# One tanh result left in its PSUM bank, and a list plan that knows the shared SBUF port

## Chip, core and metric

The kernel runs on one core of a Trainium2 chip. The metric is the device time of one execution in microseconds. PE is TensorE (matmuls), DVE is VectorE, ACT is ScalarE, POOL is GpSimd, and SP is the engine whose queue issues nearly all transfers (DMA).

## The reference, cut to what matters

The input x has 64 batches of 256 nodes with 128 features, in fp32. Four graph layers follow each other, each wrapped as a residual with a layernorm. All share one symmetric 256 x 256 adjacency matrix.

```
x = layernorm(x + attention0(x, adj))      # softmax over axis 1, plus x @ self_weight
x = layernorm(x + attention1(x, adj))      # softmax over masked leaky scores, then elu
x = layernorm(x + gated(x, adj, steps=5))  # see below
x = layernorm(x + chebyshev(x, adj, 3))    # adj^1, adj^2, adj^3 times x, then a weight

# one of the five steps of gated(); in_matrix and out_matrix are both adj
m_in = m_out = adj @ h
av = concat(m_in, m_out)
u3 = h @ u3_w.T + u3_b
z  = sigmoid(av @ w3_w.T + w3_b + u3)
r  = sigmoid(av @ w4_w.T + w4_b + u3)
hv = tanh(av @ w5_w.T + w5_b + ((r * h) @ u5_w.T + u5_b))
h  = (1 - z) * h + z * hv
```

## The kernel before, in words

**Units and lanes.** Two batches make a unit, so there are 32 units. Ten lanes, each with its own SBUF tiles, hold ten units in flight at once. A unit goes through `layer0` to `layer3` in its lane, and when it is done the lane starts the unit ten further on.

**A state update (layer2).** A unit's five updates each do the following.

1. `left_fast` multiplies by the adjacency in a scheme with seven block products in place of eight. `block_sums` (L833, L835, L836) forms sums of blocks, for these layers on GpSimd. Two banks, `x` and `y`, take the products (PE L844). Two small ScalarE copies (L856 and L859, 128 x 128) stand inside this chain, since a copied partial result is accumulated further in the same bank. Then VectorE merges (L865, and L875, L877, L878 in `merged`) into the tile m.
2. `product` (PE L902) adds up the gate inputs in the bank `ps_g` and those of candidate v in the bank `ps_v`, both 512 columns wide.
3. ScalarE takes three tanh: r's (L914), z's (L922), candidate v's (L931). Sigmoids are written through tanh with scales, so no table changes.
4. VectorE does four `scalar_tensor_tensor`: r times h (L917), (z - 1) times h (L929), (z + 1) times v (L933), and the difference that is the new state (L935). Here v is the product of candidate v.
5. The new state is turned back to node-major form. For most steps VectorE transposes 32 x 32 blocks (L943), SP writes the result to the HBM buffer hb (L946) and reads it back in another order into ht (L949, four transfers). At the first and last units some turns go through TensorE (L968) and a ScalarE copy (L971).

In the groups of the profile, r and z stand under the tile name e and v under p, because they share those tiles' memory.

**Other lines named below.** L351 are warm-up matmuls. In `layer0` and `layer1`: L576 spreads a row to all partitions with TensorE, L667 and L743 are matmuls of layer 0, L674 and L698 small and wide VectorE steps, L773 masks the attention weights and L780 uses them, L783 and L792 follow. L533 turns x by TensorE and L535 copies it out. L546, L549 and L552 turn x through HBM. L592 is the power -0.5 on GpSimd in every layernorm, L611 the normalisation on ScalarE. L314 loads x, L654 transposes it for later units. L821 are plain adjacency products. L1004 and L1015, and at the last three units L1051, L1055 and L1058, belong to layer 3. L629 to L642 are the layernorm and the output of the last units.

**The order.** No engine's order is written by hand. `Plan.add` records every operation as a task, with an engine, an estimated duration in ns, and the cells it reads and writes. `Plan.run` then goes through a planned time: each engine, when free, takes from its ready tasks the one with the smallest key, and the instructions are issued in that order. Each engine then executes its own list strictly in order, and semaphores hold an instruction until its inputs are there. So the plan's times only set the order; the run's times are the chip's.

What shapes the order:

- `LATENCY` is added after a task before a task on another engine may count on it; `EARLY` takes its place in the first 35 us of planned time. `OWN` is the same for a task on its own engine.
- The eight PSUM banks are handed out by the plan. A task that takes a bank is only chosen when one is free, and a bank is free when its last user has ended.
- The key `first` is the unit's number times `PERIOD` plus the task's due time within its unit, which `PACE` (or `PACE_GATED` in layer 2) stretches. For the last ten units `LATE` and `TAIL` bring the units closer together. `HASTE` is taken off the key of a task that uses a bank without taking it.

Of the kernel before, what the change touches and what calls it, by code (L numbers as in the profile page):

```python
# [13 lines left out]
P = 128  # L14
# [6 lines left out]
BL = 32  # L21
# [11 lines left out]
PERIOD = 46000.0  # L33
TAIL = 0.3
LATE = 6
PACE = 3.0
PACE_GATED = 1.65
HOLD = 80
DIRECT_ROWS = 3
XDIRECT = 10  # L40
START = 35e3
HASTE = {"pe": 10000.0, "act": 10000.0, "dve": 10000.0}
PLAIN = 3
# [17 lines left out]
class Task:  # L61
    def __init__(self, eng, ns, fn, unit, wait, dma):
        self.eng, self.ns, self.fn, self.unit, self.wait, self.dma = eng, ns, fn, unit, wait, dma
        self.step, self.layer = 0, 0
        self.deps, self.then, self.left, self.at = set(), [], 0, 0.0
        self.off = self.end = self.due = 0.0
        self.banks, self.takes = [], []


class Plan:  # L70
# [4 lines left out]

    LATENCY = {"pe": 500, "dve": 400, "act": 400, "pool": 500, "sp": 3500}

# [9 lines left out]

    def add(self, eng, ns, fn, reads=(), writes=(), after=(), wait=0, group=None, dma=False):
        t = Task(eng, ns, fn, self.unit, wait, dma or eng == "sp")
        for c in reads:  # L90
            t.deps.update(c.writers)
            c.readers.append(t)
        for c in writes:
            if c.bank and not c.writers:
                t.takes.append(c)
            if group is None or c.group is not group:
                c.waits = {w for o in (c, *c.over) for w in (*o.writers, *o.readers)} - {t}
                c.writers, c.readers, c.group = [], [], group
            t.deps.update(c.waits)
            if c.bank and c.writers:  # L100

                t.deps.add(c.writers[0])
            c.writers.append(t)
        t.deps.update(after)
        t.deps.discard(t)
        for c in {id(c): c for c in (*reads, *writes) if c.bank}.values():
            c.users += 1
            t.banks.append(c)
        t.step = self.step = self.step + 1
        t.layer = self.layer  # L110
        t.rank = self.rank
        self.tasks.append(t)
        return t

    def seen_at(self, t, by):
        return t.end if t.eng != by.eng or t.dma else t.off + self.OWN[t.eng]

    def run(self, spawn, units, key):

        queue, done_at, order = list(units), {}, []  # L120
        open_units, lane_of = {}, {}
        ready = {e: [] for e in ("pe", "dve", "act", "pool", "sp")}
        free = dict.fromkeys(ready, 0.0)
        seen, now, running = 0, 0.0, []

# [15 lines left out]
        def start(lane):  # L141
            mine = [u for u in queue if u % LANES == lane]
            if mine:
                self.unit, self.step = mine[0], 0
                queue.remove(self.unit)
                lane_of[self.unit] = lane
                spawn(self.unit, lane)

                for t in self.tasks[seen:]:
                    t.due = max([d.due + (PACE_GATED if t.layer == 2 else PACE) * (d.ns + (  # L150
                        d.wait + self.LATENCY["sp" if d.dma else d.eng] if d.dma or d.eng != t.eng else self.OWN[t.eng]))
                        for d in t.deps if d.unit == t.unit], default=0.0)
                enlist()

# [3 lines left out]
        while any(ready.values()) or running:  # L158
# [10 lines left out]
            for e, tasks in ready.items():  # L169
# [4 lines left out]
                if not fit:  # L174
                    continue
                t = min(fit, key=key)
                if t.at > now:
# [4 lines left out]
                order.append(t)  # L182
                free[e] = t.off = now + t.ns
                t.end = t.off + (self.EARLY if now < START else self.LATENCY)["sp" if t.dma else e] + t.wait
# [19 lines left out]
def kernel(  # L204
# [315 lines left out]
    def small(u, what, ns, op, reads, writes, **more):  # L520

        pool = u >= TIGHT and what in SMALL
        add(POOL if pool else DVE, 300 if pool else ns, lambda: op(nc.gpsimd if pool else nc.vector), reads, writes, **more)

# [55 lines left out]
    def layernorm(u, L, pairs, swap=False, centred=False):  # L580
# [5 lines left out]
        for k, (c, view) in enumerate(pairs):  # L586
# [4 lines left out]
            op0=ALU.mult, op1=ALU.add), (st,), (ve,))  # L591
        add(POOL, 1150, lambda: nc.gpsimd.tensor_tensor(rstd.ap, ve.ap, nhalf.ap, op=ALU.pow), (ve, nhalf), (rstd,))  # L592
        by_act = u >= TIGHT and plan.layer in NORM

        if by_act and not centred:
            mean = st.ap.rearrange("p k (j s) -> p k j s", j=2)[:, :, :, 1]
            if "shift" in SMALL:
                add(POOL, 330, lambda: nc.gpsimd.tensor_scalar_mul(
                    nm.ap.rearrange("p (k j) -> p k j", k=2), mean, -1.0), (st,), (nm,))
                add(POOL, 250, lambda: nc.gpsimd.tensor_mul(ve.ap, nm.ap, rstd.ap), (nm, rstd), (ve,))  # L600
            else:
# [47 lines left out]
    def layer0(u, L):  # L649
# [47 lines left out]
        for b in range(UB):  # L697
            add(DVE, 540, lambda b=b: nc.vector.tensor_add(  # L698
                ev[:, b, :, 0:P].rearrange("p k (c i) -> p k c i", c=NC), rv()[:, b].rearrange("p c (i k) -> p k c i", k=2),
                neg0.ap[:, :, 0:P].rearrange("p k (c i) -> p k c i", c=NC)), (row, neg0), (e,), group=es)  # L700
        for b in range(UB):
# [22 lines left out]
        if not SCALES or u < TIGHT:  # L724
            add(DVE, 700, lambda: nc.vector.tensor_mul(
                h.ap[:, :, 0 : D + 2], h.ap[:, :, 0 : D + 2],
                rs.ap.rearrange("p (g o) -> p g o", o=1).to_broadcast([P, G, D + 2])), (h, rs), (h,))
        esd, rstd = L["esd"], L["rstd"]
# [27 lines left out]
    def layer1(u, L):  # L756
# [6 lines left out]
        for bs in [[b] for b in range(UB)] if u < HALVES else [list(range(UB))]:  # L763
# [3 lines left out]
            for b in bs:  # L767
# [6 lines left out]
                p.ap[:, at].rearrange("p (b c) n -> p b (c n)", b=n), e.ap[:, at].rearrange("p (b c) n -> p b (c n)", b=n),  # L774
                mask1.ap.rearrange("p (o c) n -> p o (c n)", o=1).to_broadcast([P, n, NC * N])), (ec, mask1), (pc,))

# [34 lines left out]
        xf = X[u].ap.rearrange("p b c d -> p (b c d)")  # L811
        add(DVE, 600, lambda: nc.vector.scalar_tensor_tensor(hp.ap, ex.ap, 1.0, hp.ap, op0=ALU.min, op1=ALU.max), (ex, hp), (hp,))
        add(DVE, 630, lambda: nc.vector.tensor_add(hp.ap, hp.ap, xf), (hp, X[u]), (hp,))
        layernorm(u, L, y_pairs(hp))


# [8 lines left out]
    def block_sums(src, blk, s, by_pool):  # L825
# [4 lines left out]
        by, eng = (POOL, nc.gpsimd) if by_pool else (DVE, nc.vector)  # L830
        wide, narrow = (780, 580) if by_pool else (350, 215)

        add(by, wide, lambda: eng.tensor_sub(  # L833
            four[:, 0:2], blk(slice(2, 3)).to_broadcast([P, 2, D]), blk(slice(0, 4, 3))), (src,), (s,), group=ss)
        add(by, narrow, lambda: eng.tensor_sub(four[:, 2:3], four[:, 1:2], blk(slice(0, 1))), (src, s), (s,), group=ss)  # L835
        add(by, narrow, lambda: eng.tensor_add(four[:, 3:4], four[:, 2:3], blk(slice(1, 2))), (src, s), (s,), group=ss)  # L836
        return four
# [42 lines left out]
    def layer2(u, L):  # L880
        h, ht = turned(u, L, -1), X[u]
        for step in range(STEPS):
# [18 lines left out]
            def product(ps, w, c, rhs, start, stop, after=()):  # L901
# [11 lines left out]
            up = part if step else 1.0  # L913
            add(ACT, 590, lambda ps_g=ps_g, up=up: nc.scalar.activation(  # L914
                r.ap, ps_g.ap, AF.Tanh, bias=bias2.ap[:, 1:2], scale=0.5 / up), (ps_g, bias2), (r,))
            tanh_r = list(r.writers)
            add(DVE, 650, lambda h=h: nc.vector.scalar_tensor_tensor(r.ap, r.ap, 1.0, h.ap, op0=ALU.add, op1=ALU.mult),  # L917
                (r, h), (r,))
            product(ps_v, lambda: gT.ap[:, 2], gT, m, True, False, tanh_r)
            product(ps_g, lambda: gT.ap[:, 0], gT, m, False, True)  # L920
            product(ps_v, lambda: u5T.ap[:, 0], u5T, r, False, True)
            add(ACT, 590, lambda ps_g=ps_g, up=up: nc.scalar.activation(  # L922
                z.ap, ps_g.ap, AF.Tanh, bias=bias2.ap[:, 0:1], scale=0.5 / up), (ps_g, bias2), (z,))

            new = L["xT1" if h is L["xT0"] else "xT0"]
            if not step:
                add(ACT, 600, lambda h=h, new=new, part=part: nc.scalar.mul(new.ap, h.ap, part), (h,), (new,))
                h = new
            add(DVE, 650, lambda h=h, new=new: nc.vector.scalar_tensor_tensor(  # L929
                new.ap, z.ap, -1.0, h.ap, op0=ALU.add, op1=ALU.mult), (z, h), (new,))  # L930
            add(ACT, 590, lambda ps_v=ps_v, up=up: nc.scalar.activation(  # L931
                v.ap, ps_v.ap, AF.Tanh, bias=bias2.ap[:, 2:3], scale=1 / up), (ps_v, bias2), (v,))
            add(DVE, 650, lambda: nc.vector.scalar_tensor_tensor(v.ap, z.ap, 1.0, v.ap, op0=ALU.add, op1=ALU.mult),  # L933
                (v, z), (v,))
            add(DVE, 650, lambda new=new, part=part: nc.vector.scalar_tensor_tensor(  # L935
                new.ap, v.ap, part, new.ap, op0=ALU.mult, op1=ALU.subtract), (v, new), (new,))
            h = new
# [35 lines left out]
        if far(u, STEPS - 1):  # L973
            add(DVE, 600, lambda: nc.vector.tensor_add(
                y.ap.rearrange("p (g a i) -> p g a i", g=G, i=BL), ht.ap.rearrange("p (a g i) -> p g a i", g=G, i=BL),
                X[u].ap.rearrange("p b c (a i) -> p (b c) a i", i=BL)), (ht, X[u]), (y,))
        else:
# [99 lines left out]
    def first(t):  # L1077
        if t.rank is not None:
            return t.rank * PERIOD
        if t.unit < 0:  # L1080
            return t.due - 1e6
        soon = HASTE.get(t.eng, 0) if t.banks and not t.takes else 0
        return (t.unit if t.unit < NU - LANES else NU - 1 - LATE - (NU - 1 - t.unit) * TAIL) * PERIOD + t.due - soon

# [33 lines left out]
```

The softmax here doesn't subtract the row's maximum and nothing guards it: scores larger than these inputs give would overflow.

## Time and profile before

| | |
|---|---|
| median of 5 runs | 1388.79 us (1388.35 to 1391.1) |
| the profiled execution | 1388.35 us, its span 1386.4 us |
| TensorE clock granted | 0.999 |
| busy, share of span | PE 99%, DVE 86%, ACT 68%, POOL 45% |
| transfers | 47.1% of 16 DMA engines on the main queue, 105 GB/s of HBM traffic |

The span runs from the first to the last instruction of the profile; about 2 us of the execution's own time lie around it. A matmul of fp32 stands as two rows in the profile (a transpose by TensorE as one)[...]. The interval from one row's start to the next one's tells what TensorE is really occupied with. In a groups line the first number is the busy time, the second the mean duration in ns, and what follows the bar is the idle time of the engine just before. A line of waits names the waiting engine and line, the one waited for, the total us, the number of times, and the longest.

### The profile page before, as it was taken

The numbers are of one execution on the slowest core, as the hardware profiler recorded it, in microseconds if no ns is written. First come the engines' busy times: TensorE is split into PE (matmuls) and PEld (weight loads), VectorE is DVE, ScalarE is ACT, GpSimd is POOL, SyncE is SP. The second block draws the span as 40 slices with busy tenths as digits, with TensorE's granted clock in tenths as the row PEclk, the third lists the DMA queues.
The fourth block names the chain that finished last, engine by engine and source line by source line (L and its number), as shares of the span: only waits on it lengthen the run. The fifth ranks groups of instructions, "written<-read, shape, count | busy, mean of one in ns | idle before, by whom it ended". The sixth has DMA issues, their size and how long they took to land.

```text
span 1386.4 us, 23294 instructions
## 1 busy us (share of the span) xinstructions
PE 1378.4 (99%) x6891; PEld 965.9 (70%) x6891; DVE 1195.2 (86%) x2745; ACT 943.0 (68%) x2303; POOL 626.5 (45%) x1039
## 2 busy tenths in 40 slices
PE   9999999999999999999999999999999999999998
PEld 8776666766666766676776777777676666667777
DVE  7888898998888898888988798899888888998865
ACT  6887556665766777766687678887766655565544
POOL 4134343534355454455354454465444533535433
PEclk9999999999999999999999999999999999999999
DMA  4224544554555554554545555445454454554322
GB/s 132 35 50 101 117 105 105 113 124 111 113 119 108 110 127 101 120 114 107 116 108 115 118 118 117 107 112 121 107 131 97 104 108 94 113 124 114 82 65 61
DMA packets 530077, 147.13 MB, mean 106 GB/s; under 512 B 456480, under 2 KB 495136, under 8 KB 529952
## 3 DMA queue, kind: packets, MB, share of 16 engines
q1 hardware_dynamic: 529152, 145.13, 47.1%
q8 instruction: 55, 0.90, 0.3%
q14 instruction: 70, 0.57, 0.2%
q10 hardware_dynamic: 800, 0.52, 0.1%
HBM read 81.10 MB, written 64.46 MB: 105 GB/s over the span
## 4 chain that ended last, share of the span: by engine, by line
PE 95%; DVE 3%; issue 0%; DMA 0%; POOL 0%; ACT 0%; SPq 0%; POOLq 0%; DVEq 0%; ACTq 0%
PE ps L902 48%; PE ps L844 20%; PE ps L1004 7%; PE ps L743 4%; PE ps L780 4%; PE ps L1015 3%; PE ps L738 2%; PE ps L667 2%; PE ps L792 2%; PE ps L821 1%; PE ps L1051 1%; DMA ht<-hb 0%; PE ps L1058 0%; DVE p L546 0%; PE ps L351 0%
## 5 line engine op out<-in xcount | busy, mean ns | idle before, releaser
L902 PE MATMUL ps<-m,gT 128*128 128x512 f32 x960 | 478.8, 593 | 0.0
L902 PEld LDWEIGHTS ps<-m,gT 128*128 128x128 f32 x960 | 166.0, 191 | 113.1 <-issue 91.1
L833 POOL TENSOR_TENSOR e<-ht 128x256 f32<-128x256 f32 x121 | 102.3, 845 | 213.6 <-DMA ht<-hb 160.1
L844 PEld LDWEIGHTS ps<-adjTp,ht 128*128 128x128 f32 x726 | 124.0, 191 | 82.5 <-issue 72.4
L914 ACT ACTIVATE e<-ps,bias 128x512 f32<-128x512 f32 x160 | 109.8, 686 | 95.2 <-PE ps L902 90.7
L931 ACT ACTIVATE p<-ps,bias 128x512 f32<-128x512 f32 x160 | 109.7, 685 | 85.6 <-PE ps L902 82.5
L902 PE MATMUL ps<-e,u5T 128*128 128x512 f32 x320 | 163.2, 593 | 0.0
L592 POOL TENSOR_TENSOR rstd<-ve,nhalf 128x4 f32<-128x4 f32 x126 | 143.1, 1137 | 36.3 <-DVE ve L589 31.3
L589 POOL TENSOR_SCALAR ve<-st 128x4 f32<-128x4 f32 x110 | 38.3, 349 | 258.4 <-DVE st L587 230.2
L844 PE MATMUL ps<-adjTp,e 128*128 128x128 f32 x968 | 149.6, 275 | 0.0
L922 ACT ACTIVATE e<-ps,bias 128x512 f32<-128x512 f32 x160 | 109.8, 687 | 55.4 <-PE ps L902 55.2
L844 PEld LDWEIGHTS ps<-adjTp,e 128*128 128x128 f32 x968 | 130.5, 192 | 13.8 <-issue 11.1
L844 PE MATMUL ps<-adjTp,ht 128*128 128x128 f32 x726 | 138.9, 275 | 0.2 <-DMA ht<-hb 0.2
L933 DVE SCALAR_TENSOR_TENSOR p<-e,p 128x512 f32<-128x512 f32 x160 | 114.1, 714 | 20.1 <-ACT p L931 19.5
L902 PEld LDWEIGHTS ps<-e,u5T 128*128 128x128 f32 x320 | 58.9, 190 | 63.8 <-issue 49.3
L611 ACT ACTIVATE x<-ht,ve,rstd 128x128 f32<-128x128 f32 x212 | 92.3, 489 | 14.0 <-POOL ve L600 14.0
L902 PE MATMUL ps<-xT,gT 128*128 128x512 f32 x192 | 98.0, 593 | 0.0
L875 DVE TENSOR_TENSOR m<-ps,m 128x256 f32<-128x256 f32 x182 | 74.8, 411 | 18.6 <-PE ps L844 17.3
L833 POOL TENSOR_TENSOR e<-x 128x256 f32<-128x256 f32 x61 | 48.6, 797 | 92.0 <-ACT x L611 78.6
L769 ACT ACTIVATE e<-m,esd 128x256 f32<-128x256 f32 x116 | 84.3, 767 | 0.2 <-DMA m<-row 0.2
L917 DVE SCALAR_TENSOR_TENSOR e<-e,xT 128x512 f32<-128x512 f32 x96 | 67.9, 708 | 16.5 <-ACT e L914 15.7
L844 PEld LDWEIGHTS ps<-adjT,x 128*128 128x128 f32 x366 | 60.7, 191 | 29.2 <-issue 24.3
(211 smaller groups left out, 3198.8 us busy)
## 6 DMA issues: line engine op xcount, KB each, us to landing
hb<-p SPq DMA_DIRECT2D x182, 256.0 KB, 2.4
ht<-hb SPq DMA_DIRECT2D x484, 64.0 KB, 2.5
xT<-hb SPq DMA_DIRECT2D x244, 64.0 KB, 2.6
m<-row SPq DMA_DIRECT2D x58, 256.0 KB, 3.8
hb<-p SPq DMA_DIRECT2D x124, 64.0 KB, 1.8
ht<-hb SPq DMA_DIRECT2D x31, 256.0 KB, 2.9
out_dram<-x SPq DMA_DIRECT2D x30, 256.0 KB, 2.5
m<-in_x_dram SPq DMA_DIRECT2D x88, 64.0 KB, 2.4
```

Source lines behind the costliest of these rows:

```text
L592: add(POOL, 1150, lambda: nc.gpsimd.tensor_tensor(rstd.ap, ve.ap, nhalf.ap, op=ALU.pow), (ve, nhalf), (rstd,))
L611: add(ACT, 400, lambda j=j, b=b, ch=ch, view=view, at=at, shift=shift, col=col: nc.scalar.activation(X[u].ap[:, b, ch, :], view()[:, j, :] ...
L769: add(ACT, 660 if u >= DIRECT_ROWS else 360, lambda g=g, b=b: nc.scalar.activation(e.ap[:, g, :].rearrange("p (c n) -> p c n", c=NC), ev() ...
L833: add(by, wide, lambda: eng.tensor_sub(four[:, 0:2], blk(slice(2, 3)).to_broadcast([P, 2, D]), blk(slice(0, 4, 3))), (src,), (s,), group=ss)
L844: add(PE, mm_ns(P) + 4, lambda: nc.tensor.matmul(ps.ap[:, at * P : (at + 1) * P], lhs(), mat.ap[:, k, c * P : (c + 1) * P], start=start, s ...
L875: add(DVE, 335, lambda: nc.vector.tensor_tensor(mv[:, 1:3], pv(y)[:, 0:2], mv[:, 3:4].to_broadcast([P, 2, P]), op=ALU.add), (y, m), (m,))
L902: add(PE, mm_ns(T), lambda: nc.tensor.matmul(ps.ap, w(), rhs.ap, start=start, stop=stop, skip_group_check=True), (c, rhs), (ps,), after)
L914: add(ACT, 590, lambda ps_g=ps_g, up=up: nc.scalar.activation(r.ap, ps_g.ap, AF.Tanh, bias=bias2.ap[:, 1:2], scale=0.5 / up), (ps_g, bias2 ...
L922: add(ACT, 590, lambda ps_g=ps_g, up=up: nc.scalar.activation(z.ap, ps_g.ap, AF.Tanh, bias=bias2.ap[:, 0:1], scale=0.5 / up), (ps_g, bias2 ...
L931: add(ACT, 590, lambda ps_v=ps_v, up=up: nc.scalar.activation(v.ap, ps_v.ap, AF.Tanh, bias=bias2.ap[:, 2:3], scale=1 / up), (ps_v, bias2), ...
L933: add(DVE, 650, lambda: nc.vector.scalar_tensor_tensor(v.ap, z.ap, 1.0, v.ap, op0=ALU.add, op1=ALU.mult), (v, z), (v,))
L1004: add(PE, mm_ns(N), lambda k=k, src=src, c=c, b=b, ps=ps, at=at: nc.tensor.matmul(gd(ps.ap)[:, at], bn(src.ap)[:, b, c * P : (c + 1) * P], ...
```

## The change

**Candidate v's tanh.** `IN_PSUM = (0, 0, 1, 0)` says for four values of an update (r's tanh, z's tanh, v's tanh, v's product) whether they stay in PSUM. Only the third does: ScalarE's tanh (L931 before, L968 after) writes over its own bank `ps_v` in place of the SBUF tile v. VectorE's product (L933 before, L971 after) reads the bank and writes the tile v. In the text of the update the last product into `ps_g` now stands ahead of the first product into `ps_v`.

**The plan.** Tasks have a mark `port` where VectorE reads two tensors of SBUF, and every GpSimd task has it. The plan starts a marked task on one of the two engines only when the other's marked task has let go. `TURN` puts a second marked VectorE task in a row behind unmarked ones whose keys are within 1000. VectorE's durations in units are multiplied by 1.03.

**Reserves, pace and haste.** `LATENCY` is shorter for pe, dve and act and longer for pool and sp. `HASTE` is now also taken off pool and sp tasks. It no longer goes to all tasks that use a bank without taking it, but to those that lie, in their unit's chain of dependences, between two uses of one bank (`hold`). `PACE`, `PACE_GATED`, `TAIL` and `LATE` have other values. Estimated durations are set anew: GpSimd's small steps at 180 to 195, its power at 1010, its sums at 705 and 435, VectorE's updates at 600.

The matrices, the tiling, the split of work between the engines and which turns go through HBM are the same. Cut to its core:

```diff
-TAIL = 0.3
-LATE = 6
-PACE = 3.0
-PACE_GATED = 1.65
+TAIL = 0.4
+LATE = 5
+PACE = 4.0
+PACE_GATED = 1.8
...
-HASTE = {"pe": 10000.0, "act": 10000.0, "dve": 10000.0}
+HASTE = {"pe": 10000.0, "act": 10000.0, "dve": 10000.0, "pool": 10000.0, "sp": 10000.0}
+IN_PSUM = (0, 0, 1, 0)
+MARGIN = {"dve": 1.03}
+TURN = 1000.0
...
-    LATENCY = {"pe": 500, "dve": 400, "act": 400, "pool": 500, "sp": 3500}
+    LATENCY = {"pe": 400, "dve": 350, "act": 350, "pool": 700, "sp": 4000}
...
+    def hold(self, tasks):
+        bits = {}
+        for t in tasks:
+            own = 0
+            for c in t.banks:
+                own |= bits.setdefault(id(c), 1 << len(bits))
+            t.after = t.before = own
+        for t in tasks:
+            for d in t.deps:
+                if d.unit == t.unit:
+                    t.after |= d.after
+        for t in reversed(tasks):
+            for d in t.deps:
+                if d.unit == t.unit:
+                    d.before |= t.before
+        for t in tasks:
+            t.within = bool(t.after & t.before) and not t.takes
...
-                t = min(fit, key=key)
+                t = min(fit, key=lambda t: key(t) + (TURN if twice and t.port and e == "dve" else 0))
...
-                free[e] = t.off = now + t.ns
+                begin = now
+                if t.port:
+                    begin = max(now, held["pool" if e == "dve" else "dve"])
+                free[e] = t.off = begin + t.ns
+                if e == "dve":
+                    twice = t.port
+                if t.port:
+                    held[e] = t.off - 65 if e == "dve" else begin + 50 if t.ns > 900 else t.off - 125
...
-        wide, narrow = (780, 580) if by_pool else (350, 215)
+        wide, narrow = (705, 435) if by_pool else (335, 211)
...
-            product(ps_v, lambda: gT.ap[:, 2], gT, m, True, False, tanh_r)
             product(ps_g, lambda: gT.ap[:, 0], gT, m, False, True)
+            product(ps_v, lambda: gT.ap[:, 2], gT, m, True, False, tanh_r)
...
+            tz, tv = ps_g if IN_PSUM[1] else z, ps_v if IN_PSUM[2] else v
...
-            add(ACT, 590, lambda ps_v=ps_v, up=up: nc.scalar.activation(
-                v.ap, ps_v.ap, AF.Tanh, bias=bias2.ap[:, 2:3], scale=1 / up), (ps_v, bias2), (v,))
-            add(DVE, 650, lambda: nc.vector.scalar_tensor_tensor(v.ap, z.ap, 1.0, v.ap, op0=ALU.add, op1=ALU.mult),
-                (v, z), (v,))
+            add(ACT, 590, lambda ps_v=ps_v, up=up, tv=tv: nc.scalar.activation(
+                tv.ap, ps_v.ap, AF.Tanh, bias=bias2.ap[:, 2:3], scale=1 / up), (ps_v, bias2), (tv,))
+            vv = (v, ps_g, ps_v)[IN_PSUM[3]]
+            add(DVE, 600, lambda tz=tz, tv=tv, vv=vv: nc.vector.scalar_tensor_tensor(
+                vv.ap, tz.ap, 1.0, tv.ap, op0=ALU.add, op1=ALU.mult), (tv, tz), (vv,), port=not (IN_PSUM[1] or IN_PSUM[2]))
...
-        soon = HASTE.get(t.eng, 0) if t.banks and not t.takes else 0
+        soon = HASTE.get(t.eng, 0) if t.within else 0
```

## The prediction

> **What bounds the kernel now.** I read the page's busy times first, then the TensorE clock, then the chain that ended last, then TensorE's own waits.
>
> ```profile
> PE 1378.4 (99%) x6891; PEld 965.9 (70%) x6891; DVE 1195.2 (86%) x2745; ACT 943.0 (68%) x2303; POOL 626.5 (45%) x1039
> ...
> PEclk9999999999999999999999999999999999999999
> ...
> PE 95%; DVE 3%; issue 0%; DMA 0%; POOL 0%; ACT 0%; SPq 0%; POOLq 0%; DVEq 0%; ACTq 0%
> ```
>
> TensorE (PE) is busy for 99% of the span at full clock, and it is 95% of the chain. But a row lasts longer than the interval to the next row, so "busy" can hide small stalls. The chain in order of time gives the intervals:
>
> ```profile
> 1.34 3.78 PE ps L351 x8
> ...
> 145.72 4.29 PE ps L902 x10
> ...
> 156.50 3.12 PE ps L844 x28
> ...
> 1372.32 3.45 PE ps L1058 x16
> ```
>
> Ten 512-column rows take 4.29, so one takes 0.429 us. A 128-column row takes 3.12/28 = 0.111 and a 256-column row 3.45/16 = 0.216. By the medians of all start-to-start intervals in the trace, 1600 rows of 512 (686.4), 900 of 256 (194.4), 4365 of 128 to 133 (489.2 at 0.112 to 0.113) and 26 tiny ones (3.0) need **1373.0 us**. The first matmul starts at 1.34 and the last at 1380.44. Packed without a gap, the last would start at 1.34 + 1373.0 - 0.216 = 1374.1. So 6.3 us are lost on TensorE. Of these 2.05 are the eight warm-up rows (3.78 less 8 x 0.216). About 4.2 us are stalls, and 5.9 us follow the last matmul's start.
>
> ```profile
> PE ps L351 <- POOL ident masks.py:199: 1.3, 1, 1.3
> PE ps L780 <- DVE p L773: 0.5, 1, 0.5
> PE ps L576 <- DVE cu L674: 0.2, 1, 0.2
> PE ps L667 <- DVE xT L654: 0.2, 1, 0.2
> PE ps L844 <- DMA ht<-hb: 0.2, 1, 0.2
> ```
>
> These are all of TensorE's visible waits (the first is the start). By intervals the largest stalls are 0.63 (L773, at 37.3), 0.38 (L674, at 15.9), 0.33 (L654, at 1110.9), 0.33 (the landing of ht, at 292.6), 0.20 (a copy L856, at 384.3), 0.19 (at 1378.6) and 0.15 (L878, at 160.3). Ten small ones, 0.04 to 0.12 each, stand behind the ScalarE copies L856 and L859 and the tanh L914 (nine of all these are the copies'). After each stall the next rows are another 0.07 to 0.10 late.
>
> **What the Trainium skill says.** "Perfetto Trace Analysis", Identifying the Most-Contended Engine, warns that matmul busy share is no measure of headroom; the trace agrees, which is why I used intervals. "SBUF — State Buffer", Who interferes with whom: VectorE and GpSimd share one port pair as an exclusive lock, and a VectorE instruction with two SBUF inputs contends. The trace agrees:
>
> ```profile
> L933 DVE SCALAR_TENSOR_TENSOR p<-e,p x160: 642/682/1217, 50.8 to 1355.4; 128x512 f32<-128x512 f32 x160
> ...
> L833 POOL TENSOR_TENSOR e<-ht x121: 717/730/1708, 91.6 to 1302.7; 128x256 f32<-128x256 f32 x121
> ```
>
> (min/median/max ns.) Equal shapes take up to twice or more their median. "ScalarE: Activation LUTs", Step-by-step: what each stage is for, says that ScalarE writes PSUM faster than SBUF; no row of before writes a tanh there.
>
> **The change part by part.** Both programs, as built, hold the same instructions: 3507 matmuls, 1416 transfers on SP's queue, 2745 VectorE rows, the same GpSimd and ScalarE work. So 1373.0 us stands, and only stalls, the start and the tail can move. All queues are reordered from about 6 us on.
>
> (1) *Candidate v in PSUM.* 160 tanh (L931) write the bank instead of SBUF, 160 products (L933) read it. For ScalarE I take 0 from 0.687 us each; bounds +0.05 and -0.05, so +-8 us of an engine at 68%. For the product the nearest row with one PSUM operand is L978 with 0.691, against 0.714 mean for L933: about 160 x 0.02 = 4 us less VectorE time, and 160 x 0.7 = 110 us in which the port stays free. GpSimd's L833 has a mean of 829 against a median near 731, so 182 x 0.1 = 18 us of port blocking stand there. All this lies beside TensorE. What can reach it is lateness: VectorE and GpSimd run less behind the plan, which I value at a quarter of the copies' stalls (nine at 0.18 with what follows, 1.6 us): **-0.4**; bounds 0 and -1.6. The bank is held longer, until the product is done. In the built order 48 matmuls wait for such a product, where 21 waited for the tanh; the least TensorE work between is 3.28 us. Tanh, product and the next VectorE step together took 2.5 to 3.2 us (L931, L933, L935), the first two about 0.7 less. So 0. Past that, about 1 us of extra queueing, every matmul behind the waiting one would be late with it.
>
> (2) *Longer reserves for transfers and GpSimd* (sp 3500 to 4000, pool 500 to 700), port holders apart, and haste on POOL and SP. I measured in both orders the matmul time standing between the matmul that feeds a chain and the one that waits for it. The shortest transposing round through HBM has 15.11 us (14.38 before), with GpSimd's sums behind it 18.20 (17.40). So transfers and GpSimd operations moved past one another come no later for TensorE. The stalls at 292.6 and 1110.9 (0.40 each with what follows) and the VectorE ones at 160.3 and 284.6 (0.25, 0.18) should go: **-1.2**; bounds 0 and -1.2.
>
> (3) *Shorter reserves for pe, dve, act* (500/400/400 to 400/350/350). A trip matmul, ScalarE copy, matmul has 0.15 less. L856 and L859 need 0.46 after the matmul plus 0.05 for the signal. Trips with 0.91 us or less number 25 before and 51 after (four with 0.45); 9 small stalls would be 18. 9 x 0.18 = 1.6; I take half, since ScalarE's lateness is partly VectorE's: **+0.8**; bounds 0 and +7.6 (all 51 stall: 9.2 less 1.6). The tanh L914 to the next product needs 0.89 + 0.05; its second percentile is 1.35 (1.52 before), enough.
>
> (4) *The new order at the start.* At 45.1 us one such tanh has only 0.45: stall 0.5 + 0.1 = +0.6. Unit 1's attention product has 4.15 us behind its transposes (4.47 before, which stalled 0.63): +0.3. The second L674 has 2.29 (2.06 before, stall 0.38): -0.25. **+0.65**; bounds -1 and +2.
>
> (5) *The tail* (TAIL, LATE, PACE). The last nine matmuls are the same and so is the 0.43 us in front of L1058 (the 0.19 stall). Unit 31's final layernorm has 7.46 us of cover (7.87 before), and took 5.77. The 5.9 us after the last matmul stay: **0**; bounds -0.5 and +1.
>
> (6) VectorE gets 86 more wait-only instructions, ScalarE 43 fewer; at the 17 ns of ScalarE's median one, 1.5 us off the path. 0.
>
> Sum: -0.4 - 1.2 + 0.8 + 0.65 = -0.15. The profiled execution took 1388.35 (span 1386.4 and 1.95 around it), so 1388.2; the median of the runs is 0.44 above it: **1388.6**.
>
> **The rivals.** *Faster:* every removable stall goes. That is 4.2 less the 0.19 at the end: 1388.79 - 4.0 = 1384.8. For it: the plan's costs come nearer to the rows. Against: L914 at 45.1 and the first units' chains are short in the order itself. *Slower:* the shorter reserve decides. If two thirds of the 51 short copy trips stall, 34 x 0.18 = 6.1 replaces 1.6, with (4) and less the gains of (1) and (2): 1388.79 + 4.5 + 0.65 - 1.6 = 1392.3. It decides from about 16 more stalls than the gains pay for. For it: TensorE has no other slack, so each late copy shows. Against: 16 of the 25 such trips before did not stall. *The change doesn't do what it says:* port holders still collide, since the order is fixed and engines drift; then GpSimd's mean stays near 829, TensorE does not notice, and the time is 1388.8.
>
> **How the numbers follow.** About 0.2% (2.8 us) is what a measurement of this kernel can tell from no change. To be faster by that, over two thirds of the removable 4.0 us must go with nothing new: 0.08. To be slower by that needs the second rival: 0.16. The rest, 0.76, is the sum above or the ineffective change. The range runs from 1385.6, short of the full removal, to 1392.6, the slower rival's value and a little over.
>
> **What would show it.** Right: 1373.0 us of rows again; first matmul near 1.3; 3 to 6 us of stalls; a stall near 45 us behind the r tanh; more PE or PEld waits behind the copies (now L891, L894), fewer behind transfers; the product of v (L971) near 690 ns with fewer long rows; GpSimd's wide sum (L868) below 829 on average. Wrong: rows that need more than 1373 us, stalls of over 8 us, a stall pattern on the product of v or on a bank, or a tail other than 5.9 us.

## The result, and the profile after

The median of 26 runs is **1386.60 us** (1385.88 to 1387.12). In the same comparison 46 runs of the kernel before have a median of 1389.36 (1387.72 to 1391.11). The ratio is 0.9979 with a 95% interval of 0.9973 to 0.9984: 2.8 us less, about 0.2%. The runs of after also spread less, over 1.2 us against 3.4. The execution that was profiled took 1386.20 us.

The page of after, in the parts shown of before: the busy times, the clock, the chain by engine.

```profile
PE 1376.8 (99%) x6891; PEld 966.4 (70%) x6891; DVE 1185.9 (86%) x2745; ACT 946.2 (68%) x2303; POOL 588.4 (43%) x1039
...
PEclk9999999999999999999999999999999999999999
...
PE 98%; DVE 1%; DMA 0%; SPq 0%; POOL 0%; issue 0%; POOLq 0%; ACT 0%; DVEq 0%; ACTq 0%
```

Nothing here looks like a cause: PE is still 99% of the span. VectorE is 9.3 us less busy and GpSimd 38.1. The chain in order of time has the same intervals as before (ten rows of 512 in 4.29, sixteen of 256 in 3.45):

```profile
1.34 3.72 PE ps L386 x8
138.21 4.29 PE ps L937 x10
...
177.99 3.45 PE ps L1042 x16
```

By intervals the rows need 1373.0 us again, the first starts at 1.34 and the last at 1378.45 (1380.44 before). The span is 1384.4 (1386.4), so the tail is again 5.9. The gaps between rows, rows that start later than their shape's median interval allows, add up to 5.9 us, against 7.9. (The prediction's 6.3 is smaller because rows that start a little early are taken off there; counted that way the loss falls from 6.3 to 4.3.) By stretch:

| gaps between TensorE's rows, us | before | after |
|---|---|---|
| to 6 us (warm-up rows) | 2.09 | 1.96 |
| 6 to 70 us | 1.83 | 1.52 |
| 70 to 1300 us | 3.72 | 2.12 |
| last part | 0.30 | 0.31 |

So the 2.0 us between the two profiled executions are gaps, and 1.6 of them lie in the long middle. TensorE's own visible waits, all there are in after:

```profile
PE ps L386 <- POOL ident masks.py:199: 1.3, 1, 1.3
PE ps L611 <- DVE esd L783: 0.6, 1, 0.6
```

The waits for the attention weights, for x's turn and for ht's landing are gone from this list; one behind a small VectorE product at 47.4 us (L783, a gap of 0.72) is new. Most short stalls show at the weight loads. The lines "who waited for it" of the copy that was L856 and is L891, before and then after:

```profile
PEld ps L844: 5.2, 15
```

```profile
PEld ps L879: 2.9, 10
PEld ps L937: 0.5, 2
```

Fewer waits, though the order leaves more copies a short trip. A wait of a weight load is not yet lost time of the matmuls, though: x9 below, with before's order, has 5.1 us of such waits behind this copy, as many as before, and yet smaller gaps. And the two operations of candidate v (min/median/max ns), the tanh of before first, then the two of after:

```profile
L931 ACT ACTIVATE p<-ps,bias x160: 665/687/762, 49.6 to 1354.7; 128x512 f32<-128x512 f32 x160
...
L968 ACT ACTIVATE ps<-ps,bias x160: 623/662/690, 52.3 to 1351.0; 128x512 f32<-128x512 f32 x160
...
L971 DVE SCALAR_TENSOR_TENSOR p<-e,ps x160: 633/677/690, 53.4 to 1352.0; 128x512 f32<-128x512 f32 x160
```

The tanh's median is 25 ns shorter. The product's longest is 690 where it was 1217: with one operand in PSUM none of the 160 was held up. GpSimd's wide sum, the groups of after (busy us, mean ns):

```profile
L868 POOL TENSOR_TENSOR e<-ht 128x256 f32<-128x256 f32 x121 | 99.2, 820 | 119.7 <-DMA ht<-hb 72.6 <-PE ps L937 19.3 <-PE ps L879 18.1
...
L868 POOL TENSOR_TENSOR e<-x 128x256 f32<-128x256 f32 x61 | 47.3, 776 | 87.8 <-ACT x L646 76.2 <-DVE x L654 6.3 <-PE ps L702 3.1
```

Before it took 845 ns from ht and 797 from x.

### The profile page after: what moved, and what is told of

Read it like the earlier page. It is cut to its first block, busy times and chain, and to the rows that moved or that the text cites. A ratio compares the mean times of both kernels' runs of the same rounds, so it can differ in the third digit from the quotient of the medians.

```text
span 1384.4 us, 23333 instructions
## 1 busy us (share of the span) xinstructions
PE 1376.8 (99%) x6891; PEld 966.4 (70%) x6891; DVE 1185.9 (86%) x2745; ACT 946.2 (68%) x2303; POOL 588.4 (43%) x1039
## 4 chain that ended last, share of the span: by engine, by line
PE 98%; DVE 1%; DMA 0%; SPq 0%; POOL 0%; issue 0%; POOLq 0%; ACT 0%; DVEq 0%; ACTq 0%
PE ps L937 50%; PE ps L879 21%; PE ps L1042 7%; PE ps L778 4%; PE ps L815 4%; PE ps L1053 3%; PE ps L827 2%; PE ps L773 2%; PE ps L702 2%; PE ps L856 1%; PE ps L1089 1%; PE ps L568 0%; PE ps L1096 0%; PE ps L386 0%; PE ps L1006 0%; DMA u<-rowu 0%
## 5 line engine op out<-in xcount | busy, mean ns | idle before, releaser
L937 PE MATMUL ps<-m,gT 128*128 128x512 f32 x960 | 471.9, 593 | 0.0
L937 PEld LDWEIGHTS ps<-m,gT 128*128 128x128 f32 x960 | 169.5, 191 | 132.2 <-issue 116.2
L968 ACT ACTIVATE ps<-ps,bias 128x512 f32<-128x512 f32 x160 | 105.2, 659 | 91.7 <-PE ps L937 86.9
L624 POOL TENSOR_SCALAR ve<-st 128x4 f32<-128x4 f32 x110 | 34.7, 315 | 278.6 <-DVE st L622 272.7
L868 POOL TENSOR_TENSOR e<-ht 128x256 f32<-128x256 f32 x121 | 99.2, 820 | 119.7 <-DMA ht<-hb 72.6
L971 DVE SCALAR_TENSOR_TENSOR p<-e,ps 128x512 f32<-128x512 f32 x160 | 107.8, 676 | 27.5 <-ACT ps L968 26.9
L646 ACT ACTIVATE x<-ht,ve,rstd 128x128 f32<-128x128 f32 x212 | 93.9, 491 | 1.4 <-POOL ve L635 1.4
L708 POOL COPY cu<-ht 128x12 f32<-128x12 f32 x28 | 9.9, 355 | 196.5 <-ACT ht L705 196.1
```

The lines of the kernel that those rows point to most:

```text
L646: add(ACT, 400, lambda j=j, b=b, ch=ch, view=view, at=at, shift=shift, col=col: nc.scalar.activation(X[u].ap[:, b, ch, :], view()[:, j, :] ...
L868: add(by, wide, lambda: eng.tensor_sub(four[:, 0:2], blk(slice(2, 3)).to_broadcast([P, 2, D]), blk(slice(0, 4, 3))), (src,), (s,), group=s ...
L937: add(PE, mm_ns(T), lambda: nc.tensor.matmul(ps.ap, w(), rhs.ap, start=start, stop=stop, skip_group_check=True), (c, rhs), (ps,), after)
L968: add(ACT, 590, lambda ps_v=ps_v, up=up, tv=tv: nc.scalar.activation(tv.ap, ps_v.ap, AF.Tanh, bias=bias2.ap[:, 2:3], scale=1 / up), (ps_v, ...
L971: add(DVE, 600, lambda tz=tz, tv=tv, vv=vv: nc.vector.scalar_tensor_tensor(vv.ap, tz.ap, 1.0, tv.ap, op0=ALU.add, op1=ALU.mult), (tv, tz), ...
```

## The experiments

Five theories were put against each other. A: the plan's new reserves and port model make the gain. B: the bank and the port that it frees make it. C: any new order of instructions moves the time by a us or more. D: of the plan, the port model rather than the reserves. E: at a given order the bank is worth little, and orders make the rest. Each kernel was timed next to the kernel before on the same chip, x1 to x8 on one chip and x9 to x12 on another; ratios are to that, with 95% intervals. Before's median was 1389.88 us beside x1 to x4, 1390.12 beside x5 to x8 and 1390.28 beside x9 to x12, so a time in us cannot be set directly beside the 1389.36 and 1386.60 above; the ratio can.

### The bank alone in the old plan, and the new order without the bank

x1 is before with the bank alone (the plan knows it, so its order changes too). x2 is after with every engine's order kept, but the tanh through SBUF: only the functions change, not what the plan sees.

```diff
# x1, in before
-                v.ap, ps_v.ap, AF.Tanh, ...), (ps_v, bias2), (v,))
+                ps_v.ap, ps_v.ap, AF.Tanh, ...), (ps_v, bias2), (ps_v,))
-  ... scalar_tensor_tensor(v.ap, z.ap, 1.0, v.ap, ...), (v, z), (v,))
+  ... scalar_tensor_tensor(v.ap, z.ap, 1.0, ps_v.ap, ...), (ps_v, z), (v,))
# x2, in after
-                tv.ap, ps_v.ap, AF.Tanh, ...), (ps_v, bias2), (tv,))
+                v.ap, ps_v.ap, AF.Tanh, ...), (ps_v, bias2), (tv,))
-  ... scalar_tensor_tensor(vv.ap, tz.ap, 1.0, tv.ap, ...), (tv, tz), (vv,), ...
+  ... scalar_tensor_tensor(vv.ap, tz.ap, 1.0, v.ap, ...), (tv, tz), (vv,), ...
```

> The kernel before with one part alone: candidate v's tanh stays in its bank, old plan and constants. Theory A (the new reserves and port model of the plan make the gain, the bank hardly): within 1.5 us of before, 1388 to 1390.5; VectorE's product near 690 ns as after, GpSimd's wide sum some 15 ns shorter on average. Theory B (the bank and the freed port make it): 1386 to 1387.5, ratio about 0.998, with TensorE's lost time down to 4 us. Theory C (any new order moves the time by a us or two): anything from 1386.5 to 1391.

> The kernel after with its order of instructions kept exactly on every engine, but candidate v's tanh written to SBUF and read from there. It takes the hardware's share of the bank away and leaves the plan's. Theory A: within 0.7 us of after, at most 1387.3, though the product's mean goes back from 676 to about 710 ns and GpSimd's sums are longer. Theory B: at least half of the gain is lost, 1388 or more, with new stalls of TensorE behind VectorE or GpSimd. Theory C: as A, since the order is the same.

Measured: x1 1387.49, ratio 0.9983 (0.9977 to 0.9990). x2 1387.29, ratio 0.9980 (0.9972 to 0.9987). Each part alone has nearly the whole gain of 0.9979. Theory A misses x1 and theory B misses x2; theory C misses neither. The parts do not add up to 5 us, so they seem to remove the same kind of loss. In x2 VectorE and GpSimd are as busy as before,

```profile
PE 1377.2 (99%) x6891; PEld 966.4 (70%) x6891; DVE 1199.4 (87%) x2745; ACT 947.9 (68%) x2303; POOL 623.0 (45%) x1039
```

13.5 and 34.6 us more than after with the same order, yet its ratio hardly differs (the intervals leave room for about 1 us). Busy time of these two is not what sets the time in this order.

### The bank at the old order, and x1's order without the bank

x9 is the mirror of x2: before in its exact order, with the tanh in PSUM. x10 is x1's exact order with the tanh through SBUF.

```diff
# x9, in before: the functions of x1, but the plan's cells stay (ps_v, bias2), (v,) and (v, z), (v,)
+                ps_v.ap, ps_v.ap, AF.Tanh, ...), (ps_v, bias2), (v,))
+  ... scalar_tensor_tensor(v.ap, z.ap, 1.0, ps_v.ap, ...), (v, z), (v,))
# x10, in x1: the functions of before, the cells of x1
+                v.ap, ps_v.ap, AF.Tanh, ...), (ps_v, bias2), (ps_v,))
+  ... scalar_tensor_tensor(v.ap, z.ap, 1.0, v.ap, ...), (ps_v, z), (v,))
```

> The kernel before in its exact order, with candidate v's tanh written to its bank and read from there: the hardware's share of the bank alone, the mirror of x2. The plan does not know it, so a matmul may find its bank held by the product for longer. Theory E (at a given order the bank is worth under a us; the orders make the rest): 1388.5 to 1389.8, with product and GpSimd's sums shorter as in x1. Theory B (the bank's relief makes x1's gain): 1387 to 1388, as x1.

> The exact order of x1, but the tanh through SBUF: what x1's order is worth without the bank. Theory E: 1387.3 to 1388.6, most of x1's 2.4 us stays. Theory B: 1389 or more, as before.

Measured: x9 1387.65, ratio 0.9981 (0.9974 to 0.9989), 2.6 us below before. x10 1389.42, ratio 0.9996 (0.9987 to 1.0004), no change that shows. So theory E falls, and B holds for these orders of the old plan: at before's exact order the bank alone takes 2.6 us, which no luck of the order can explain, and at x1's it takes about 1.8 (0.9983 against 0.9996, with intervals that overlap a little). At after's order (x2) it takes next to nothing. Nor does the bank make any order good: x7, x8 and x12 below have it and are slower than before. The page of x9, and its product's and GpSimd's lines:

```profile
PE 1376.0 (99%) x6891; PEld 966.1 (70%) x6891; DVE 1186.4 (86%) x2745; ACT 942.0 (68%) x2303; POOL 604.9 (44%) x1039
```

```profile
L933 DVE SCALAR_TENSOR_TENSOR p<-e,ps x160: 642/677/690, 50.3 to 1353.6; 128x512 f32<-128x512 f32 x160
...
L833 POOL TENSOR_TENSOR e<-ht x121: 717/731/1784, 90.9 to 1300.3; 128x256 f32<-128x256 f32 x121
```

VectorE is busy 8.8 us less than before and GpSimd 21.6. Not every operation of GpSimd is shorter: the wide sum from ht, which theory E too expected shorter, takes 858 ns on average against 845, and most of the saving lies in the narrow sums and the power. TensorE's gaps tell where the time went, in one execution each; the profiled one of x9 was its fastest of 16 (1386.56 us). There the gaps behind the copies L856 and L859 are 0.35 (0.98 before), those behind L654, L878, L917 and L914 are gone (0.71 together), and so is that behind ht's landing (0.33). One of 1.28 stands behind GpSimd, at 284.7 us:

```profile
PE ps L844 <- POOL e L835: 1.1, 1, 1.1
```

There the narrow sum L835 took 1324 ns (median 458) while VectorE's mask product L773, with two operands in SBUF, ran beside it for 1427. In before L773 started after that sum had ended. The same order on every engine can still collide or not.

### How much is luck of the order

Three kernels change a reserve by 1 or 2 ns; nothing else changes but the order into which the list plan falls.

```diff
# x3, in before
-    LATENCY = {"pe": 500, "dve": 400, "act": 400, "pool": 500, "sp": 3500}
+    LATENCY = {"pe": 500, "dve": 400, "act": 401, "pool": 500, "sp": 3500}
# x11, in before
+    LATENCY = {"pe": 500, "dve": 400, "act": 400, "pool": 500, "sp": 3502}
# x4, in after
-    LATENCY = {"pe": 400, "dve": 350, "act": 350, "pool": 700, "sp": 4000}
+    LATENCY = {"pe": 400, "dve": 350, "act": 351, "pool": 700, "sp": 4000}
```

> The kernel before with ScalarE's reserve 401 in place of 400 ns, which no theory of mechanism can feel; it only reshuffles the last two thirds of TensorE's order. Theories A and B: 1388.5 to 1390, the same as before. Theory C: a change of 1 us or more in either direction.

> The kernel before with the reserve after transfers 3502 in place of 3500 ns. It reshuffles all five queues (a third to more than half of each) from 170 to 200 us on and nothing else. Theory C (part of the gain is luck of the order): a change of over 1 us in either direction from before. Theories B and E: before's time to within 0.7 us.

> The kernel after with ScalarE's reserve 351 in place of 350 ns, which only reshuffles its order. Theories A and B: 1386.0 to 1387.3, the same as after. Theory C: a change of 1 us or more, the more likely upwards.

Measured: x3 1390.02, ratio 0.9998 (0.9990 to 1.0007). x11 1392.71, ratio 1.0015 (1.0008 to 1.0022): **2 ns in one reserve cost 2.4 us**. x4 1387.55, ratio 0.9983 (0.9976 to 0.9990), about 0.6 us above after by the ratio, with overlapping intervals. How far the nudges really reached is in the traces. In x3 only 14 of TensorE's 6891 rows stand at another place than in before (by line and tile), so it is nearly before once more and no draw of a new order; what its expectation calls a reshuffle is mostly other bank numbers. In x11 2996 rows stand elsewhere. So theory C holds in one of the two nudges that gave a new order: orders of one plan can lie 2.4 us apart. TensorE's largest waits in x11 after the start:

```profile
PE ps L844 <- POOL e L835: 1.2, 1, 1.2
PE ps L902 <- DVE m L878: 0.8, 1, 0.8
PE ps L780 <- DVE p L773: 0.7, 1, 0.7
PE ps L844 <- ACT e L856: 0.6, 1, 0.6
```

The first has no counterpart in before's list, and the trace shows how it came about. At 1256.65 us GpSimd began a narrow sum L835 that took 3453 ns where the median is 457. In that time VectorE ran five products of two SBUF operands (L929, L933, L929, L935, L933), each starting before the last had ended, and the sum ended 0.3 us after the last of them. Here five holders of the port came in a row.

### Parts of the plan

```diff
# x5, in before
+    LATENCY = {"pe": 500, "dve": 400, "act": 400, "pool": 700, "sp": 4000}
# x6, in x2
+    LATENCY = {"pe": 400, "dve": 350, "act": 350, "pool": 500, "sp": 3500}
# x7, in after
-        t.port = port or eng == "pool"
+        t.port = False
```

> The kernel before with two numbers alone: the reserves after transfers and GpSimd are 4000 and 700 ns as after (3500 and 500). The shortest round through HBM gets 15.32 us of matmuls (14.38), the one with GpSimd's sums behind it 18.16 (17.40). Theory A (TensorE's stalls come from these chains being late; longer reserves remove them): ratio 0.9985 or lower, 1388 or less. Theory D (the port model with its new durations is what makes the plan true; the reserves alone do little): within 1 us of before. Both are beside the point if the time rises.

> The kernel after without its bank part (tanh through SBUF, as in x2) and with the reserves after transfers and GpSimd back at 3500 and 500; the port model, the new durations, the shorter reserves of the other engines and pace and tail stay. Chains have 14.23 and 16.88 us. Theory A: most of the gain is gone, 1388.5 or more, with stalls behind transfers or GpSimd. Theory D: it stays near x2, at most 1387.8.

> The kernel after with no task marked as holding the port, so that the plan neither delays nor spreads the holders; everything else as after. GpSimd's wide sum should be longer on average than after (820 and 776 ns), towards 845. Theory A: within 1 us of after. Theory D: 1388.3 or more.

Measured: x5 1393.77, ratio 1.0025 (1.0016 to 1.0034). x6 1391.39, ratio 1.0012 (1.0005 to 1.0018). x7 1391.71, ratio 1.0010 (1.0002 to 1.0018). The longer reserves alone made before slower by 3.7 us, which neither A nor D had expected. Putting them back cost about 4 us from x2 to x6; A had the time, but not its reason (after the start TensorE's longest waits there are behind ScalarE steps and a VectorE step, none behind a transfer or GpSimd), and D missed it. Leaving out the port model cost about 0.3% against after, which D had and A missed. All three are larger than the 2.4 us that 2 ns made in x11, but with so few orders tried none can be credited to its edit with certainty. In x7 GpSimd's wide sum takes 859 ns from ht and 812 from x on average, against 820 and 776 in after.

```profile
L868 POOL TENSOR_TENSOR e<-ht 128x256 f32<-128x256 f32 x121 | 103.9, 859 | 115.1 <-DMA ht<-hb 55.9 <-PE ps L937 23.2 <-PE ps L879 22.9
L868 POOL TENSOR_TENSOR e<-x 128x256 f32<-128x256 f32 x61 | 49.6, 812 | 71.7 <-ACT x L646 62.4 <-DVE x L654 4.5 <-DVE rs L831 3.8
```

After's neighbour x4, with the model, has 835 and 775; x1 and x9, with the bank but the old plan, have 829 and 858 from ht, 803 and 792 from x. So the sum from x is 15 to 37 ns shorter wherever the model is on beside the bank. For the sum from ht the ranges overlap, and that the model shortens it is not shown.

### The reserves of the engines, in both directions

```diff
# x8, in after
+    LATENCY = {"pe": 300, "dve": 200, "act": 200, "pool": 700, "sp": 4000}
# x12, in after
+    LATENCY = {"pe": 500, "dve": 400, "act": 400, "pool": 700, "sp": 4000}
```

> The kernel after with the reserves of pe, dve and act cut once more, to 300, 200 and 200. The rival of the prediction that ends slower: copy trips of at most 0.91 us number 115 (51 after, 25 before), 24 of them under 0.5, and the tanh of r to its product has 1.12 in the shortest tenth against a need of 0.94. If each short trip costs some 0.18 us in a third of the cases, the time is 6 us above after, 1392; if ScalarE is as punctual as the small stalls of after say (nine behind copies of 51 trips), about 20 stalls and 1389; if the reserve has no effect, 1386.6.

> The kernel after with the reserves of pe, dve and act back at 500, 400 and 400 (x8 went the other way). 41 copy trips of at most 0.91 us instead of 51. Step (3) of the prediction: 0.8 us below after, 1385.8, which would beat both kernels. Theory C: anything between 1385.5 and 1390. If longer reserves only push other work later: above after by 1 us or more.

Measured: x8 1399.68, ratio 1.0068 (1.0055 to 1.0080), more than any of the three values given. The loads behind the copy L891 waited 32 times for 10.7 us (10 for 2.9 in after), the shape that was expected, and the gaps behind the two copies, with the late rows after them, come to about 5 us. But the largest stall was another, at 182.6 us behind a merge of VectorE:

```profile
PE ps L879 <- DVE m L913: 3.4, 1, 3.4
PE ps L386 <- POOL ident masks.py:199: 1.3, 1, 1.3
PE ps L1096 <- ACT e L1093: 1.1, 1, 1.1
```

With what follows it until 191 us this one place holds 5.9 us of gaps; from 187.7 the granted clock was 0.5 for 3.4 us. So of the 13 us by which x8 is slower than after, under half are what the prediction's rival described.

x12 1403.15, ratio 1.0089 (1.0076 to 1.0103). It does not test what it was made for: of its 23.2 us of gaps 15.3 lie at the end, and only 3.1 between 70 and 1300. The order brings the last units' work too late. From 1375.3 us on TensorE waits behind x of L646 (2.6) and the copy L891 (1.2); at 1379.7 its granted clock falls to 0.5 for 13.7 us; and in that time it waits 4.0 us more for a transfer, from about 1383.4:

```profile
PE ps L1089 <- DMA xT<-hb: 4.0, 1, 4.0
PE ps L879 <- ACT x L646: 2.6, 1, 2.6
```

```profile
1300.00:1375.00 75.00, 74.77 (x351) 53.71 (x350) 49.44 (x112) 39.23 (x89) 25.02 (x54) 1.00 0.27 63
1375.00:1396.00 21.00, 12.76 (x42) 9.65 (x40) 4.74 (x14) 3.50 (x10) 3.17 (x6) 0.67 0.16 37
```

(PE, PEld, DVE, ACT, POOL busy, then the clock.) None of the twelve has a lower ratio than after.

## Why the prediction held, and where its steps were off

The frame was right. The same instructions ran, the rows needed 1373.0 us, only gaps moved, the tail stayed at 5.9, and the time lies in the range. The likeliest case was not: 1388.6 said no change, and the result is 2.8 us below before; to be faster by that much or more it had given 0.08. So the range held by its width, not because the sum was right. Step by step:

- *Step (1), the bank:* a gain by punctuality was rightly forecast, its size was not. The term was -0.4, with bounds of 0 and -1.6. At before's order it measures -2.6 us (x9), beyond the bound, because I let it reach only the copies' stalls. In x9 the gaps behind VectorE, behind x's load and behind ht's landing went as well. That VectorE and GpSimd, less often late, serve every chain and not one is how I read this; it rests on one execution of each kernel. At after's order the same term is near nothing (x2).
- *Step (2), longer reserves:* the four stalls named are gone in after, as summed (-1.2). That the reserves did it is not shown: alone they made before slower (x5).
- *Step (3), shorter reserves:* +0.8 cannot be read off after alone. After has nine gaps behind the two copies, as before, and 1.02 us in them against 0.98, though 51 short trips stand where 25 stood. But after also has the bank. With the placement of the tanh held fixed, the new order has more: 1.02 against 0.35 (x9) with the bank, and about 1.2 (x2) against 0.98 through SBUF. That is +0.7 and +0.2 in single executions, so a cost of this sign was there, and the bank hid it.
- *Step (4), the start:* +0.65 measured as -0.3 (1.83 to 1.52). The tanh with only 0.45 us showed no stall of its own, since TensorE was held just ahead of the product that needed it, at 47.4, by the small product L783 (0.72). So a stall of about the forecast size came at that place, from a wait that step (4) did not name. Unit 1's attention product, expected 0.3 worse than its 0.63, came only 0.10 late. A distance in the order is a risk, not a stall.
- *Steps (5) and (6):* 0 and 0, as found.
- *The sum:* steps were added as if independent. The bank at before's order and the new plan without it each remove about 2.6 us, and both together 2.8. Why they stop there is not shown: after still has about 2 us of gaps between 70 and 1300 us.
- *The base:* 1388.79 was the median of five runs; 46 runs give 1389.36. The low base took 0.6 us off the miss. The profiled execution, at 1388.35, was low among them, so a typical run probably had about one us more of stalls than the page showed.
- *Signs of being right:* 3 to 6 us of stalls were expected; in the prediction's own count (4.3 lost, of which 2.0 are warm-up rows) 2.3 are left. The waits of loads behind the copies became fewer, not more.
- *One reading of the lines:* not every stall is followed by 0.07 to 0.10 us more. Of 30 stalls of at least 0.03 us in before past 6 us, 19 were, within two rows.

The faster rival named the right quantity, stalls that vanish, and after took 2.8 of its 4.0 us by the medians, 2.0 in the profiled executions. The slower rival did not happen at this dose; x8 is in part what it looks like. The ineffective change is refuted by the time, by the product's longest of 690 ns and by the wide sum's mean of 805 over all 182 (829 before).

**What stays open.** How much of the new plan's own gain (x2) comes from its port model, its reserves or its pace, and how much from landing on a good order, since 2 ns move the old plan by 2.4 us. With the tanh in SBUF the old plan's constants gave ratios of 0.9996 (x10), 0.9998 (x3), 1 and 1.0015 (x11), none near x2's 0.9980; but of the new plan that is one order, and more neighbours of both would be needed to separate a better plan from a better draw. Moving the tanh also did two things at once, and no run parts them: the product left the port free, and ScalarE's tanh became 25 ns shorter. Which of the stalls the bank removes is read from one execution of each kernel, not from all.

## What to carry to other kernels

When one engine is packed to 99%, sum the start-to-start intervals of its rows: that gives the floor, and floor plus head and tail bounds any gain before a line of the change is read. Two changes that both make the helpers more punctual need not add up (here 2.6 and 2.6 gave 2.8), so test each alone and each with the order frozen: swap the operand but leave what the planner sees. And before crediting a planner's new constants, nudge one by a nanosecond or two, look in the trace whether the order really changed, and see how far chance alone moves the time.

## What the runs showed of the hardware

- A tanh of 128 x 512 fp32 from PSUM took 662 ns (median) when written to PSUM (after, x9) and 687 to SBUF (before, x2).
- A VectorE product with one operand in PSUM never took more than 690 ns over 160 instances, in after and in x9; with both in SBUF the median is 682 and the longest 1217 (before).
- A GpSimd sum of 128 x 128 took 3453 ns in x11, against a median of 457, while VectorE ran five products of two SBUF operands without a break.
- Many TensorE stalls were followed within two rows by a further delay of 0.07 to 0.10 us: 19 of 30 in before, 11 of 23 in after (stalls of at least 0.03 us past 6 us).
- In x12 TensorE's granted clock fell to 0.5 for 13.7 us, after waits of 2.6 and 1.2 us within 5 us (a mean of 0.67 over the 21 us shown); 256-column pairs then stood about 0.42 us further apart than at full clock. In x8 it fell to 0.5 for 3.4 us, soon after a wait of 3.4.
